# Layer 0's attention in written order on every engine, with the norm, the ranking and the adapter merges in other units

## The chip, the cores and the metric

The kernel runs on one core of a Trainium2 chip, in one launch. Its time is the device time of the whole launch in microseconds (us). Most of the work is matmuls on TensorE (PE). The other engines are VectorE (DVE), ScalarE (ACT), GpSimd (POOL) and SyncE (SP), which here issues the large loads and stores.

## The reference

The model has two layers, each an attention and a feed-forward part, each followed by a residual sum and a layer norm. The change lies in the first attention and in the preparation of the first feed-forward part. Eight batches of 512 rows of 512 numbers go through:

```python
x = _layernorm(x + attn0(x))        # 16 heads of 32, causal softmax, biases on Q, K, V and O
x = _layernorm(x + ffn0(x))         # 8 experts, the best 2 of each row
...
q = (x @ WQ_w.T + WQ_b); k = (x @ WK_w.T + WK_b); v = (x @ WV_w.T + WV_b)
attn = softmax(where(causal, -inf, q k^T / sqrt(32)));  out = (attn @ v) @ WO_w.T + WO_b
...
gate_delta = 2.0 * (gate_lora_B @ gate_lora_A)
probs = softmax(xf @ gate_weight.T + xf @ gate_delta.T); the top 2, their weights divided by their sum
gup = xf @ gate_up_proj[e] + 2.0 * (xf @ gup_lora_A[e].T) @ gup_lora_B[e].T
h = silu(gates) * h
out = h @ down_proj[e] + 2.0 * (h @ down_lora_A[e].T) @ down_lora_B[e].T
```

The adapters (lora A and B) have rank 16. All of it is float32. The second layer (attention with 8 heads on 2 key groups, then an integer feed-forward part) is the same code before and after the change.

## The kernel before, in words

`attention0` runs the first attention, batch by batch, b = 0 to 7. A batch has four groups g of four heads, and a group has three units u, `UNITS`: u = 0 takes the key tile 0 (512 query columns), u = 1 the key tiles 1 and 3 (384 + 128 columns), u = 2 the key tile 2 (256 columns). In each slot (g, u) the loop does the following, in this order:

1. `scores`: PE multiplies K and Q into the one buffer `sc`, ACT takes the exponential into `p`, POOL sets what lies above the diagonal to zero (affine_select).
2. the thunks that `plan(b)` has put into this slot's list.
3. `product` of the unit before (PE, `av`), and for u > 0 the adds of its p into a running sum (DVE).
4. in u = 1 `normalise` of the group before: PE sums rows (`rs`), ACT copies and bounds them (`watch_sums`), DVE takes the reciprocal and multiplies (`aoT`), POOL keeps a guard sum (`watch_inverses`, `g_total`).

The thunks of a batch b are these. `value(b, t)` in g = 0: four matmuls, and DVE adds the bias while it empties PSUM. `query` and `key` of the next group in u = 1 and u = 2: DVE empties Q, ACT empties K. `project(b - 1, t)`, t = 0 to 3, in (1,0) to (1,2): the output projection of the batch before, a DVE add to x, and after t = 3 the whole `layernorm` (statistics on DVE, the power on POOL, four subtract-and-multiply operations on DVE, four stores to `rows`). `turn(b - 1, c)`, c = 0 to 3, in (2,1) and (2,2): four transposes each on PE, the copies in turn on DVE and ACT. `score` in (3,0) and `choose` in (3,1): router logits and the top two. `dispatch(b - 2)` in (0,2): the rank of each row within its expert; `one_hot` and `enter(b - 2)` in (1,1): 24 small DVE operations of one-hot rows and a set of matmuls into a table. `merge` in (2,0) and (3,0): two adapters' deltas (`delta`, f32, 16 rows of K at row groups of 32), a scaling on ACT and an add into the expert's weights on POOL (L749, L760, L762). There are 24 merges: 12 in b1 to b6, 12 after the last batch. The load of the next x stands at g = 3 and the add of the output bias to x (one POOL operation on 128x2048) at g = 2.

PSUM for everything small (`mm`) has two buffers that alternate; `sc` has one. `one_hot` and `x1T`, the turned x, share one buffer.

The order on each engine comes from a scheduler, save where `in_order(tc)` is entered: there the order of the program is kept, for PE alone unless other engines are named. Before the change that covers the first unit, and PE from g = 2 of the last batch to the end of the tail; `begun.close()` ends the first. The tail, after the last batch, runs the first tiles of the experts (`tiles.step`, a tile of 128 rows through one expert), between them the rest of the last batch's projection, turn, score, choice, dispatch and one-hot rows, and the 12 remaining merges.

## Time and profile before

| | us |
|---|---|
| median of 3 runs | 2297.77 (2293.88 to 2298.08) |
| the profiled execution | 2295.71 |
| its span, first to last instruction | 2293.9 |
| mean granted clock | 0.994 |
| batches of layer 0's attention | 0 to about 735 |
| tail with the first expert tiles | 735 to about 850 |
| experts | to about 1190 |
| second attention | 1190 to 1776 |
| integer feed-forward part | 1780 to 2294 |

All numbers of the profile come from one execution. A line of the timeline has the start, the time from the first to the last of a group of like instructions, the engine, the line of the program, the operation, output and inputs by their names, and in brackets the idle time of the engine just before and what ended it. A matmul's own time is longer than the distance between two of them in a row, because they overlap; the cost of one is read from start to start. In windows, a row has the stretch, its length, then busy time and instructions of PE, weight loads, DVE, ACT and POOL, then the granted clock of PE, the share of DMA and GB/s.

### The profile page before, as it was taken

The page shows a single profiled execution, that of the slowest core. Times are in us where ns is not written, and L with a number is a line of the kernel's source. Part 1 is how long each engine was busy: PE and PEld are TensorE (multiplying, and loading weights), DVE is VectorE, ACT ScalarE, POOL GpSimd, SP SyncE. Part 2 cuts the span into 40 slices and gives each one's busy share as a digit, 9 for nine tenths or more (in the row PEclk, how much of TensorE's full clock was granted, in tenths as well). Part 3 has the DMA queues.
Part 4 walks back from the last instruction along what each step waited for, and adds up shares of the span by engine and source line. Part 5 has one row for each costly group of instructions (what it writes and reads, how often), then busy time and mean ns, then how long its engine had stood idle before and what let it go on. Part 6 is the DMA issues. An engine that isn't in the chain of part 4 may idle for free.

```text
span 2293.9 us, 24187 instructions
## 1 busy us (share of the span) xinstructions
PE 2240.5 (98%) x9430; PEld 1154.8 (50%) x9430; DVE 1245.0 (54%) x1974; ACT 648.2 (28%) x937; POOL 501.6 (22%) x493
## 2 busy tenths in 40 slices
PE   9999999999999999999998999999998999999997
PEld 3344444444444444444443334443343878888876
DVE  3457575666668432242216877777667544444443
ACT  2332323323324221111223323333332322222222
POOL 2231323413224231131125122321211000000000
PEclk9999999999999999999999999999999999999999
DMA  8010110101112234332233011100100100000000
GB/s 289 19 56 1 55 33 23 56 7 49 54 38 84 92 115 146 93 120 91 87 127 94 10 55 56 55 29 17 37 1 23 42 19 19 19 19 19 19 19 20
DMA packets 58444, 126.63 MB, mean 55 GB/s; under 512 B 6210, under 2 KB 6210, under 8 KB 58322
## 3 DMA queue, kind: packets, MB, share of 16 engines
q1 hardware_dynamic: 47040, 89.32, 11.1%
q0 software_dynamic: 10560, 34.61, 5.2%
q8 instruction: 77, 1.26, 0.2%
q10 hardware_dynamic: 722, 1.07, 0.1%
q14 instruction: 45, 0.37, 0.1%
HBM read 89.59 MB, written 35.39 MB: 54 GB/s over the span
## 4 chain that ended last, share of the span: by engine, by line
PE 76%; issue 8%; DVE 7%; DMA 4%; POOL 4%; ACT 2%; POOLq 0%; SPq 0%; ACTq 0%; DVEq 0%
PE ps_f L1069 7%; PE ps_g L1055 6%; PE ps_u L1055 6%; PE ps_gu L845 5%; PE ps_o L1216 5%; PE ps_o L1551 5%; PE av L1601 5%; PE sc L1579 4%; PE ps_q L1503 4%; PE ps_q L1200 4%; PE ps_k L1208 4%; PE ps_v L1193 4%; PE av L1288 3%; PE sc L1264 3%; PE ps_y L862 2%
## 5 line engine op out<-in xcount | busy, mean ns | idle before, releaser
L845 PE MATMUL ps_gu<-experts,xrT 128*128 128x512 f32 (+1 forms) x520 | 248.6, 601 | 0.0
L1268 ACT ACTIVATE p<-sc 128x2048 f32<-128x2048 f32 (+1 forms) x96 | 152.9, 1593 | 189.0 <-PE sc L1264 182.1
L1273 POOL TENSOR_SCALAR_AFFINE_SELECT p<-p 128x512 f32<-128x512 f32 x128 | 92.1, 734 | 380.1 <-ACT p L1268 376.6
L1060 DVE SCALAR_TENSOR_TENSOR hT<-ps_u,vec,sg 128x512 f32<-128x512 f32 x88 | 65.8, 748 | 201.4 <-PE ps_u L1055 201.4
L1069 PE MATMUL ps_f<-ffn_w,h_half 128*128 128x512 f32 x672 | 169.4, 392 | 1.1 <-DVE h_half L1064 1.1
L934 POOL TENSOR_TENSOR g_total<-g_total,r_inv 128x512 f32<-128x512 f32 x64 | 89.7, 1402 | 361.4 <-DVE r_inv L1612 286.2
L1612 DVE RECIPROCAL r_inv<-r_inv 128x512 f32<-128x512 f32 x32 | 106.8, 3339 | 105.4 <-ACT r_inv L931 105.4
L1582 ACT ACTIVATE p<-sc 128x1024 f32<-128x1024 f32 x128 | 124.1, 1021 | 130.3 <-PE sc L1579 119.7
L1296 DVE TENSOR_TENSOR p<-p 128x1536 f32<-128x1536 f32 (+2 forms) x96 | 129.3, 1346 | 38.5 <-POOL p L1273 21.5
L1055 PE MATMUL ps_g<-x_high,ffn_w 128*128 128x512 f32 x352 | 141.5, 402 | 3.0 <-DVE x L1557 3.0
L1069 PEld LDWEIGHTS ps_f<-ffn_w,h_half 128*128 128x128 f32 x672 | 124.5, 188 | 33.7 <-DVE h_half L1064 7.2
L848 DVE TENSOR_TENSOR h<-ps_gu,h 128x256 f32<-128x256 f32 x67 | 28.4, 424 | 205.2 <-ACT h L847 205.2
L1055 PE MATMUL ps_g<-x_low,ffn_w 128*128 128x512 f32 x352 | 139.4, 396 | 0.0
L1055 PE MATMUL ps_u<-x_high,ffn_w 128*128 128x512 f32 x352 | 139.2, 395 | 0.0
L1055 PE MATMUL ps_u<-x_low,ffn_w 128*128 128x512 f32 x352 | 139.2, 395 | 0.0
L1579 PE MATMUL sc<-qT,kT 64*128 64x512 f32 x512 | 127.9, 618 | 1.0 <-ACT qT L1505 0.7
L862 PE MATMUL ps_y<-experts,hT 128*128 128x512 f32 (+1 forms) x272 | 127.9, 592 | 0.5 <-ACT hT L856 0.5
L1200 PE MATMUL ps_q<-experts 128*128 128x512 f32 x256 | 120.4, 611 | 4.4 <-DMA experts<-in_xT 4.4
L845 PEld LDWEIGHTS ps_gu<-experts,xrT 128*128 128x128 f32 x520 | 89.6, 192 | 68.0 <-issue 68.0
L1601 PE MATMUL av<-p,v 128*64 128x512 f32 x512 | 123.8, 605 | 0.0
L1193 PE MATMUL ps_v<-experts 128*128 128x512 f32 x256 | 116.3, 602 | 2.4 <-DVE v L1195 2.4
L1208 PE MATMUL ps_k<-experts 128*128 128x512 f32 x256 | 117.5, 602 | 0.2 <-ACT r_inv L931 0.2
(256 smaller groups left out, 3544.5 us busy)
## 6 DMA issues: line engine op xcount, KB each, us to landing
results<-y SPq DMA_DIRECT2D x68, 256.0 KB
x<-in_x SPq DMA_DIRECT2D x8, 1024.0 KB
experts<-in_gate_up SPq DMA_DIRECT2D x8, 1024.0 KB
rows<-x SPq DMA_DIRECT2D x32, 256.0 KB
x<-rows SPq DMA_DIRECT2D x8, 1024.0 KB
experts<-in_xT SPq DMA_DIRECT2D x7, 1024.0 KB
out<-x SPq DMA_DIRECT2D x28, 256.0 KB
ffn_i<-in_wq_ffn SPq DMA_DIRECT2D x11, 512.0 KB
```

What stands on the lines that cost most here:

```text
L845: mm = nc.tensor.matmul(ps, lhsT=xT[:, c, :], rhs=self.weights(i, c), start=c == 0, stop=c == ND - 1)
L862: self.nc.tensor.matmul(ps, lhsT=hT[:, c, :], rhs=self.weights(i, ND + c), start=c == 0, stop=c == self.NI - 1)
L1055: nc.tensor.matmul(ps, lhsT=w[:, ts(dc, P)], rhs=x[:, dc, :], start=(dc, i) == (0, 0), stop=(dc, i) == (ND - 1, 1))
L1069: self.nc.tensor.matmul(os[t], lhsT=h[:, ts(t, P)], rhs=self.weights(2 * NHID + c), start=(c, i) == (0, 0), stop=(c, i) == (NHID - 1, 1))
L1193: nc.tensor.matmul(ps, lhsT=xts[b][:, c, ts(t, P)], rhs=wv[:, c, :], start=c == 0, stop=c == ND - 1)
L1200: nc.tensor.matmul(ps, lhsT=wq[:, g, ts(c, P)], rhs=xts[b][:, c, :], start=c == 0, stop=c == ND - 1)
L1208: nc.tensor.matmul(ps, lhsT=wk[:, g, ts(c, P)], rhs=xts[b][:, c, :], start=c == 0, stop=c == ND - 1)
L1268: nc.scalar.activation(p, sc[:, :, :width], AF.Exp, scale=scale)
L1296: nc.vector.tensor_tensor(total[:, :, P * kt :], total[:, :, P * kt :], p[:, :, at : at + w], ALU.add)
L1579: nc.tensor.matmul(sc[:, j, :], lhsT=st["kT"][hs, ts(kt, P)], rhs=st["qT"][g][hs, :], start=True, stop=True)
L1582: nc.scalar.activation(p, sc, AF.Exp, scale=scale)
L1601: nc.tensor.matmul(st["av"][HD * j : HD * (j + 1), :], lhsT=st["v"][:, kt, HD * j : HD * (j + 1)], rhs=p[:, j, :], start=kt == 0, stop=kt ...
```

## The change

Layer 0's batches 0 to 6 are written in order for PE, DVE, ACT and POOL; the last batch keeps the manner of before. With it:

- `value` is emptied by DVE and ACT in turn, without a bias. `join_bias`, once in b0, multiplies V's bias with Wo (four f32 matmuls) and adds it to the row of O's bias; the softmax's rows sum to one, so that V's bias reaches the output in this way.
- `project` takes one t a slot from (1,0) to (2,0), with its statistics; `norm` follows in (2,1). `one_hot` is cut into halves, in (1,1) and (2,1), `enter` follows (2,2)'s product. The four `turn` of a batch stand together in (3,0), `score` in (3,1), `begin_choice` in (3,2), `end_choice` in the next batch's (0,0), and `dispatch` in (0,1).
- DVE's adds of a unit come ahead of the next unit's thunks; `watch_inverses` one unit later; the O bias is added to x in four POOL operations; the load of x moves to (3,1) of the batch before.
- Adapters are fetched in 16 parts of 128 rows by up to 512 columns (256 KB) through one buffer `raw`. `split_part` puts the upper float32r half of each value (ACT) and what remains (POOL, two operations) on separate rows, so that a `delta` is one float32r matmul with K = 64. Merges come last in their slot. Splits stand in b0, b4, b7 and, four of them, in the tail, where the last merges stand two to a step.

```diff
-                nc.sync.dma_start(out=self.lora_sb[32 * j : 32 * j + R, i, :], in_=ins.lora[i, j])
+                at = 2 * P // 4 * (j % 2)
+                nc.sync.dma_start(out=self.lora_sb[32 * j : 32 * j + R, i, :], in_=ins.lora[2 * i + j // 2, at : at + R])
...
         nc.scalar.activation(tmp, tmp, AF.Exp)
+
+        yield
         nc.vector.tensor_reduce(red, tmp, AX.X, ALU.add)
         nc.vector.reciprocal(red, red)
...
-    def load_lora(self, pool, i):
-
-        self.lora = pool.tile([P, LORA], F32, tag="lora", name=f"lora_{i}")
-        for j in range(4):
-            self.nc.sync.dma_start(out=self.lora[32 * j : 32 * j + R, :], in_=self.env.ins.lora[i, j])
+    def masks(self, pool, lane):
+
+
+
+        nc = self.nc
+        bits = pool.tile([P, 2], I32, name="l_bits")
+        self.low = pool.tile([P, 2], F32, name="l_low")
+        self.sign = pool.tile([P, 2], F32, name="l_sign")
+        for i, bit in enumerate((2 * R, R)):
+            nc.vector.tensor_scalar(bits[:, i : i + 1], lane, bit, None, ALU.bitwise_and)
+        nc.vector.tensor_copy(self.low, bits)
+        nc.vector.tensor_scalar(self.low, self.low, 1.0, None, ALU.min)
+        nc.vector.tensor_scalar(self.sign, self.low, -2.0, 1.0, ALU.mult, ALU.add)
+        self.parts = [(q, c) for q in range(E // 2) for c in range(LORA_PARTS)]
+
+    def fetch_part(self, pool):
+
+        if self.parts:
+            q, c = self.parts[0]
+            at, n = 512 * c, min(512, LORA - 512 * c)
+            self.raw = pool.tile([P, 512], F32, tag="raw", name="l_raw")
+            self.nc.sync.dma_start(out=self.raw[:, :n], in_=self.env.ins.lora[q, :, at : at + n])
+
+    def split_part(self, pool):
+        nc = self.nc
+        q, c = self.parts.pop(0)
+        if c == 0:
+            self.lora = pool.tile([P, LORA], F32R, tag="lora", name=f"lora_{q}")
+        at, n = 512 * c, min(512, LORA - 512 * c)
+        i = int(c in (1, 2))
+        high = pool.tile([P, 512], F32R, tag="r_inv", name="l_high", bufs=2)[:, :n]
+        nc.scalar.activation(high, self.raw[:, :n], AF.Copy, scale=self.sign[:, i : i + 1])
+        raw = self.raw[:, :n]
+        nc.gpsimd.tensor_scalar(raw, raw, self.low[:, i : i + 1], None, ALU.mult)
+        nc.gpsimd.tensor_tensor(self.lora[:, at : at + n], raw, high.bitcast(F32), ALU.add)
+
+        if (q, c) != (E // 2 - 2, LORA_PARTS - 1):
+            self.fetch_part(pool)
 
     def delta(self, ps, e, c):
-        j = 32 * (e % 4)
-        a, bt = lora_factors(self.lora[j : j + R, :], c)
+        j = P // 2 * (e % 2)
+        a, bt = lora_factors(self.lora[j : j + P // 2, :], c)
         self.nc.tensor.matmul(ps, lhsT=a, rhs=bt, start=True, stop=True)
...
-    def step(self):
+    def step(self, amid=lambda: None):
...
+        amid()
         self.down(i)
         self.turn_rows(i + 3)
...
-        experts.load_lora(work, 0)
+        experts.masks(work, router.lane_i)
+        experts.fetch_part(work)
...
             vs[t] = own.tile([P, D], F32, tag=f"v{t}", name=f"v{t}")
-            nc.vector.tensor_tensor(vs[t], ps, row[:, 0, :], ALU.add)
+            env.evacuate(t, vs[t], ps)
+
+        def join_bias():
+
+            bv = work.tile([P, ND, P], F32, tag="r_inv", name="bv", bufs=2)
+            nc.vector.tensor_copy(bv, vec[:, V_BV : V_BV + ND, None].to_broadcast([P, ND, P]))
+            ps = mm([P, D], "ps_bias")
+            for c in range(ND):
+                nc.tensor.matmul(ps, lhsT=bv[:, c, :], rhs=wo[:, c, :], start=c == 0, stop=c == ND - 1)
+            nc.vector.tensor_tensor(row, ps, row, ALU.add)
...
             nc.vector.tensor_tensor(xs[b][:, t, :], ps, xs[b][:, t, :], ALU.add)
+            if b >= NB - 2:
+                if t == NT - 1:
+                    env.layernorm(b, router.rows[S * b : S * (b + 1)])
+                return
+            if t == 0:
+                norms[b] = [small.tile([P, NT, n], F32, name=name) for n, name in ((6, "stats"), (2, "mv"), (1, "rstd"))]
+            stats, mv, rstd = norms[b]
+            nc.vector.bn_stats(out=stats[:, t, :], in_=xs[b][:, t, :])
+            nc.vector.bn_aggr(out=mv[:, t, :], in_=stats[:, t, :])
             if t == NT - 1:
-                env.layernorm(b, router.rows[S * b : S * (b + 1)])
-
+                nc.gpsimd.tensor_scalar(rstd[:, :, 0], mv[:, :, 1], LN_EPS, None, ALU.add)
+                nc.gpsimd.tensor_tensor(rstd[:, :, 0], rstd[:, :, 0], env.neg_half, ALU.pow)
+
+        def norm(b):
+            stats, mv, rstd = norms.pop(b)
+            for t in range(NT):
+                x = xs[b][:, t, :]
+                nc.vector.tensor_scalar(x, x, mv[:, t, 0:1], rstd[:, t, :], ALU.subtract, ALU.mult)
+                nc.sync.dma_start(out=router.rows[S * b + P * t : S * b + P * (t + 1)], in_=x)
+
+        norms = {}
...
+        choosing = {}
+
+        def begin_choice(b):
+            choosing[b] = router.choose(b, logits.pop(b), mm([P, NT, E], "ps_r"))
+            next(choosing[b])
+
+        def end_choice(b):
+            next(choosing.pop(b), None)
+
         def choose(b):
-            router.choose(b, logits.pop(b), mm([P, NT, E], "ps_r"))
+            begin_choice(b)
+            end_choice(b)
...
+        def add(u, p, acc):
+            total, _ = acc
             at = 0
             for kt in UNITS[u]:
                 w = S - P * kt
-                if u:
-                    nc.vector.tensor_tensor(total[:, :, P * kt :], total[:, :, P * kt :], p[:, :, at : at + w], ALU.add)
+                nc.vector.tensor_tensor(total[:, :, P * kt :], total[:, :, P * kt :], p[:, :, at : at + w], ALU.add)
                 at += w
 
         def normalise(b, g, acc):
...
             guard.watch_sums(rs, r_inv)
             nc.vector.reciprocal(r_inv, r_inv)
             nc.vector.tensor_tensor(aoTs[b][:, g, :], av, r_inv, ALU.mult)
-            guard.watch_inverses(r_inv)
-
+            watches.append(r_inv)
...
                     todo[g, 2].append(lambda nb=nb, ng=ng: key(nb, ng))
             pb, last = b - 1, b == NB - 1
             if b:
-                places = ((1, 0), (1, 0), (1, 1), (1, 1) if last else (1, 2))
+                places = ((1, 0), (1, 0), (1, 1), (1, 1)) if last else ((1, 0), (1, 1), (1, 2), (2, 0))
                 for t, slot in enumerate(places):
-                    todo[slot].append(lambda t=t: project(pb, t))
-                places = ((2, 0),) * 4 if last else ((2, 1), (2, 1), (2, 2), (2, 2))
-                for c, slot in enumerate(places):
-                    todo[slot].append(lambda c=c: turn(pb, c))
-                todo[(2, 1) if last else (3, 0)].append(lambda: score(pb))
-                todo[(2, 2) if last else (3, 1)].append(lambda: choose(pb))
-                if not last:
-                    todo[2, 0].append(merge)
-                    todo[3, 0].append(merge)
+                    todo[slot].insert(0, lambda t=t: project(pb, t)) if not last else todo[slot].append(lambda t=t: project(pb, t))
+            if last:
+                for c in range(ND):
+                    todo[2, 0].append(lambda c=c: turn(pb, c))
+                todo[2, 1].append(lambda: score(pb))
+                todo[2, 2].append(lambda: choose(pb))
+            elif b:
+                todo[2, 1].append(lambda: norm(pb))
+                todo[3, 0] += [lambda c=c: turn(pb, c) for c in range(ND)]
+                todo[3, 1].append(lambda: score(pb))
+                todo[3, 2].append(lambda: begin_choice(pb))
+                for slot in ((2, 0), (3, 0)):
+                    after[slot] = merge
+
+            for t, slot in enumerate(((0, 0), (0, 1), (1, 0), (1, 1)) if b else ((2, 0), (2, 1), (2, 2), (3, 0))):
+                todo[slot].append(lambda t=t: nc.gpsimd.tensor_tensor(xs[b][:, t, :], xs[b][:, t, :], row, ALU.add))
+            if b + 1 < NB:
+
+                todo[3, 1].append(lambda: load_x(b + 1))
             if b == 0:
                 todo[1, 0].append(lambda: router.merge_lora(mm([P, ND, E], "ps_wr")))
+            if b == 0:
+                todo[1, 2].append(join_bias)
+            early = (0, 0), (0, 2), (1, 0), (1, 2)
+            slots = {0: ((2, 1), (2, 2), (3, 1), (3, 2)), 4: early, 7: early}
+            for slot in slots.get(b, ()):
+                todo[slot].append(lambda: experts.split_part(work))
             if b > 1:
-                todo[0, 2].append(lambda: dispatch(b - 2))
-                todo[1, 1].append(lambda: enter(one_hot(b - 2, range(NT))))
+                todo[0, 0].append(lambda: end_choice(b - 2))
+                todo[0, 2 if last else 1].append(lambda: dispatch(b - 2))
+                if last:
+                    todo[1, 1].append(lambda: enter(one_hot(b - 2, range(NT))))
+                else:
+                    todo[1, 1].append(lambda: one_hot(b - 2, (0, 1)))
+                    todo[2, 1].append(lambda: rows.append(one_hot(b - 2, (2, 3))))
+                    after[2, 2] = lambda: enter(rows.pop())
             if last:
                 todo[1, 2].append(soon)
                 todo[2, 2].append(first_rows)
...
                 todo[3, 2].append(begin)
             return todo
 
...
-        begun.enter_context(in_order(tc))
+        begun.enter_context(in_order(tc, mybir.EngineType.DVE, mybir.EngineType.Activation, mybir.EngineType.Pool))
         query(0, 0)
         key(0, 0)
         order = phase.enter_context(ExitStack())
         waiting = summing = None
         for b in range(NB):
+            if b == NB - 1:
+                begun.close()
             todo = plan(b)
             for g in range(ND):
-                if g == 2:
-                    if b + 1 < NB:
-                        load_xT(b + 1)
-
-                    nc.gpsimd.tensor_tensor(xs[b], xs[b], row[:, 1:2, :].to_broadcast([P, NT, D]), ALU.add)
-                if g == 3 and b + 1 < NB:
-                    load_x(b + 1)
+                if g == 2 and b + 1 < NB:
+                    load_xT(b + 1)
                 if b == NB - 1 and g == 1:
-                    experts.load_lora(work, 1)
                     experts.load(4)
                 if b == NB - 1 and g == 2:
                     order.enter_context(in_order(tc))
...
                 acc = []
                 for u in range(len(UNITS)):
                     p = scores(b, g, u)
+                    while watches:
+                        guard.watch_inverses(watches.pop())
+                    if waiting is not None and waiting[2]:
+                        add(*waiting[2:])
                     for thunk in todo[g, u]:
                         thunk()
-                    begun.close()
                     if waiting is not None:
-                        waiting()
+                        product(*waiting)
+                    after.pop((g, u), lambda: None)()
                     if u == 1 and summing is not None:
-                        summing()
-                    waiting = lambda b=b, g=g, u=u, p=p, acc=acc: product(b, g, u, p, acc)
-                summing = lambda b=b, g=g, acc=acc: normalise(b, g, acc)
-        waiting()
+                        normalise(*summing)
+                    waiting = b, g, u, p, acc
+                summing = b, g, acc
+        product(*waiting)
+        add(*waiting[2:])
         merge(2)
-        summing()
+        normalise(*summing)
+        guard.watch_inverses(watches.pop())
         heads_ctx.close()
         tiles.open(tiles_ctx)
         tiles.step()
...
             merge()
         for c in range(ND):
             turn(b, c)
+        experts.fetch_part(work)
         tiles.step()
         score(b)
         merge()
...
         dispatch(b)
         for places in ((0, 1), (2, 3)):
             rows = one_hot(b, places)
+            experts.split_part(work)
             tiles.step()
-            merge()
+            experts.split_part(work)
         enter(rows)
         tiles.of_fixed = router.fixed(routes)
         while merges:
-            tiles.step()
+            tiles.step(merge)
             merge()
```

More of the change, by code (lines that the diff above doesn't have):

```diff
@@ L46 @@
 LORA = 3 * 512 + 256
+LORA_PARTS = 4
 EXPERT = UPS * 512
@@ L51 @@
 WIDEST = 2048.0
-V_BQ, V_BK, V_NS, V_SS, V_SG, V_SU = 0, 4, 8, 12, 16, 16 + NHID
-N_VEC = 16 + 2 * NHID
+V_BQ, V_BK, V_NS, V_SS, V_SG, V_SU, V_BV = 0, 4, 8, 12, 16, 16 + NHID, 16 + 2 * NHID
+N_VEC = V_BV + 4
 def in_order(tc, *engines):
@@ L427, in __init__ @@
         self.tiles = numbers("r_tiles", [N_FREE], [[1, N_FREE]])
-        i = tmp.tile([P, 1], I32, name="r_lane_i")
+        self.lane_i = i = tmp.tile([P, 1], I32, name="r_lane_i")
         nc.gpsimd.iota(i, pattern=[[0, 1]], base=0, channel_multiplier=1)
@@ L1164, in attention0 @@
         load_w(wv, 0)
-        row = work.tile([P, 2, D], F32, name="row")
-        nc.sync.dma_start(out=row, in_=ins.rows.partition_broadcast(P))
+        row = work.tile([P, D], F32, name="row")
+        nc.sync.dma_start(out=row, in_=ins.rows[1].partition_broadcast(P))
         load_w(wq, 1, others)
@@ L1307, in normalise @@
             nc.vector.tensor_tensor(aoTs[b][:, g, :], av, r_inv, ALU.mult)
-            guard.watch_inverses(r_inv)
+            watches.append(r_inv)
+        watches = []
         merges = [(e, c) for e in range(0, E, 2) for c in range(UPS)]
@@ L1351, in plan @@
             return todo
+        rows, after = [], {}
         tiles = Tiles(env, router, experts.w)
@@ L1360, in begin @@
         def begin():
-            pair = work.tile([P, 2, D], F32, tag="row", name="first_turned")
-            one = work.tile([P, S], F32, tag="logits", name="first_turned")
-            tiles.begin([pair[:, 0, :], pair[:, 1, :], one], work.tile([P, 256], F32, name="first_h"),
+            rooms = [work.tile([P, S], F32, tag=tag, name="first_turned") for tag in ("row", "logits", "raw")]
+            tiles.begin(rooms, work.tile([P, 256], F32, name="first_h"),
                         lambda name: mm([P, S], name))
@@ L1993, in _layout @@
                            rows("L0_ffn_down_lora_A")], axis=3)
+    lora = np.repeat(lora.reshape(E // 2, 2, 1, R, LORA), 4, axis=2).reshape(E // 2, P, LORA)
     return {
@@ L1999, in _layout @@
             [cols(a[n]) for n in ("L0_attn_WQ_b", "L0_attn_WK_b", "L1_attn_norm_scale", "L1_attn_split_scale",
-                                  "L1_ffn_s_gate", "L1_ffn_s_up")], axis=1),
+                                  "L1_ffn_s_gate", "L1_ffn_s_up", "L0_attn_WV_b")], axis=1),
         "rows": np.stack([a["L0_attn_WV_b"], a["L0_attn_WO_b"]]),
```

## The prediction

> **What bounds the kernel now.** I read the page first: busy shares and the chain that ended last.
>
> ```profile
> PE 2240.5 (98%) x9430; PEld 1154.8 (50%) x9430; DVE 1245.0 (54%) x1974; ACT 648.2 (28%) x937; POOL 501.6 (22%) x493
> PE 76%; issue 8%; DVE 7%; DMA 4%; POOL 4%; ACT 2%; POOLq 0%; SPq 0%; ACTq 0%; DVEq 0%
> ```
>
> TensorE (PE) is busy all the time; what other engines do counts only where PE stands still for it, or where a matmul itself changes. So I went to the windows of 50 us (PE busy is the second time of a row, the granted clock the third figure from the right).
>
> ```profile
> 300.00:350.00 50.00, 49.42 (x276) 21.49 (x275) 30.32 (x35) 17.61 (x20) 13.37 (x15) 1.00 0.19 64
> 700.00:750.00 50.00, 44.92 (x252) 19.56 (x251) 39.67 (x83) 19.98 (x30) 21.91 (x23) 0.93 0.29 85
> 750.00:800.00 50.00, 48.22 (x167) 23.25 (x166) 20.62 (x59) 13.21 (x24) 14.16 (x14) 0.97 0.27 95
> ```
>
> Layer 0's batches run at full clock with 0.6 us of 50 idle: a reordering has little idle time to win there. The end of layer 0 (700 to 800) has 7 us of idle and a clock below one. Third, PE's timeline, for the stalls that there are and for the cost of one piece:
>
> ```profile
> 417.92 1.02 PE L749 MATMUL ps_lora<-lora 16*128 16x512 f32 x4
> 418.88 0.64 PE L1288 MATMUL av<-p,v 128*32 128x256 f32 x8
> 420.08 1.15 PE L1264 MATMUL sc<-q,k 32*128 32x384 f32 x16 [0.57 <-ACT p L1268]
> ...
> 463.72 2.84 PE L1193 MATMUL ps_v<-experts 128*128 128x512 f32 x6 [1.01 <-DVE v L1195]
> ...
> 699.07 1.09 PE L1228 MATMUL ps_x1T<-ident,x 128*128 128x128 f32 x8 [0.44 <-DVE g_routed L565]
> 701.11 1.15 PE L1228 MATMUL ps_x1T<-ident,x 128*128 128x128 f32 x8 [0.94 <-ACT x1T L1230]
> ```
>
> One merge of adapters takes 0.96 us from start to start; V waits 1.01 us for VectorE's (DVE's) evacuation; four transposes in a row, as the last batch has them already, stall 1.4 us. Last, DVE's timeline, for durations:
>
> ```profile
> 409.26 3.34 DVE L1306 RECIPROCAL r_inv<-r_inv 128x512 f32<-128x512 f32 x1
> 412.52 2.83 DVE L1296 TENSOR_TENSOR p<-p 128x512 f32<-128x512 f32 x2
> ...
> 419.77 4.14 DVE L153 TENSOR_SCALAR x<-x,mv,rstd 128x512 f32<-128x512 f32 x4 [1.48 <-POOL rstd L151]
> 424.90 0.75 DVE L1202 TENSOR_SCALAR q<-ps_q,vec 128x512 f32<-128x512 f32 x1 [1.00 <-PE ps_q L1200]
> ```
>
> **The batch's own sum.** Batches start (first V matmul) at 83.6, 174.4, 267.9, 360.7, 453.9, 547.9, 641.3 us: 90.7 us for b1, 93.4 as the mean of b2 to b6. From start to start in PE's timeline: V, Q, K, O 3.53 each, 16 of them 56.5; scores 1.07 + 1.08 + 0.65 by four groups 11.2; products 0.88 + 1.00 + 0.57 by four 9.8; row sums 4 x 0.98 = 3.9; rank 0.46, table 1.84, four transposes 2.1, logits 1.0, ps_r 0.89; together 87.7. Two merges are 2.22 before (eight records of two batches' 4.44). That leaves 3.4 us of 93.4: about 1.2 stalls (rows above) and about 2.1 that the transposes and merges cost over their length where the scheduler splits them among products and scores.
>
> **Merges in float32r.** Each delta becomes one record of 64 rows in place of two of 16. Price: the last layer's float32r matmul on 512 columns (L1069) repeats every 0.227 us, so a pair is estimated at 0.46 us, if the two don't overlap. Two merges 0.92: the sum is 88.65, and with 0.35 for the POOL select that PE waits for in batch 0 (61.76 us), 89.0. V's wait goes: its evacuation alternates now between DVE and ScalarE (ACT).
>
> **The turn, b2 to b6.** This is the number that decides. All four transposes now stand in (3,0), behind the table, and the table behind the norm and the second half of the one-hot rows in (2,1). DVE in its new order, from Q's end in (2,1): semaphore 0.2, q 0.7, norm four at 0.54 = 2.15, 12 one-hot operations 2.55 (24 took 5.07 from 482.40), reciprocal 3.3, aoT 0.64, adds of unit 1 2.23, table copy 0.92: 12.7 us. PE over the same stretch: product 0.88, row sums 0.98, scores 0.65, K 3.53, product 1.00, table 1.84, scores 1.07, first transpose 0.53: 10.5. With two buffers for the small products, the second transpose waits for the table's copy: 2.2 us. The third waits for the first's copy, which stands behind unit 2's add (1.17) on DVE and takes 0.68 itself; less the second's 0.53 on PE that is about 1.2. Uncontended S = 3.3. But POOL works beside DVE: the norm took 4.14 for 2.15 beside POOL, the adds 2.83 for 2.23. I take half of the norm's excess and the adds' and a little on the one-hots: S = 4.75. Ends: 1.4 (the last batch's turn, above), 6.2 (all contention in full).
>
> The clock bears on it. Here full stretches of 3.41 us at half clock follow loose ones, from 721.3, 738.4, 789.6 and 799.8 us; each costs some 1.7. A stall of 4.75 us cut by transposes is looser than anything in 50 to 700. I price one at 1.7 x 0.5 = 0.8 a batch; ends 0 and 1.7. So 89.0 + 4.75 + 0.8 = 94.55 against 93.4: +1.15 a batch, **+5.8 for five**.
>
> The Trainium skill (TensorE: Matmul & The Clock Gate, part "Why this matters for your kernels") wants no gaps over about 3 us between bursts, since one idle window of 3.4 us halves the clock. Its period agrees with the 3.41 us of the trace. The same rule taken strictly would charge the turn no clock, as transposes break the stall into 2.2 and 1.2 us, and make the sum 4 us less; the window 710 to 720, with PE 8.24 of 10 us busy, came before a halved one here, so I keep 0.8.
>
> **b1** has no table and rank, so 86.4 + 0.35 + a turn of 1.7 to 2.9 for the copies: about 89.0 against 90.7, **-1.7**.
>
> **b0.** The V bias leaves the evacuation and comes in through Wo: four f32 matmuls, 3.5 us, all on PE, with copy and add on DVE beside. In written order the three groups' 384+128 scores now wait for the 1.88 us exp in front, which Q's halves filled before: 0.73 + 1.49 + 1.49 = 3.7. Q unsplit gives 0.84 back, the select 0.35: **+6.0** (5 to 7.5).
>
> **b7, g0 and g1.** Four splits (a 256 KB load, ACT 0.6, POOL two operations of about 1.3 each by the row of the merge's add, L762). Behind the split's copy on ACT stands k's evacuation, and its part's load stands in SP's queue behind the 1 MB load of expert 4, itself waiting for PE's last V; 1 MB took 7 to 8 us at 434 us. PE then waits for k at the next score: 2 to 5 us if so, chance 0.6; with one halved stretch likely behind it **+3.5** (0 to 7). Splits in b0 and b4 have their loads an entire unit ahead: nothing, and where late, ACT would hold an exp.
>
> **The tail.** Twelve merges by 0.5: -6.0. The two merges in a burst (733.58 to 738.13, 4.55 us with two waits of 0.51) shrink by 2. One halved stretch fewer: -1.7. Against it four splits in series, each load, ACT, POOL about 6 us, ACT's hT and silu queued behind their copies: +3 (0 to 5). Merges of two a step: POOL 5.2 plus a gather 1.0 = 6.2 against a step's 5.8, some tenths. Sum **-6.7** (-14 to 0).
>
> POOL's x add in four pieces, g_total a unit later, loads of x a unit later (a whole batch of cover for a 7 to 8 us load), rows stored from the norm at 256 KB each and choice split over two units: hidden under PE's 93 us a batch, as POOL is busy 15 of 50 us; where POOL is late, the select holds the product, 0.35 a time.
>
> **Sum:** 6.0 - 1.7 + 5.8 + 3.5 - 6.7 = +6.9 on the profiled execution's 2295.7 = 2302.6. The median of runs, 2297.8, lies 2.1 higher; from midway, 2296.7, I get **2303.6**.
>
> **Rivals.**
> 1. Faster: the turn stalls no more than 3.2 us a batch, clock included, as the 1.4 at 699 us speaks for. At 1.4 each batch takes 90.4, five give -14.9, and the time is 2283; at 3.2 it is 2292. It decides below 3.2, since the other terms sum to +1.1 and 0.2% is 4.6 us. Against it: DVE's 12.7 us against PE's 10.5, which holds without any contention. Chance 0.28.
> 2. No net change: S with its clock between 3.2 and 5.1, uncontended chain or little more: 2293 to 2302. Chance 0.20.
> 3. Slower by more: contention in full and a halved stretch every batch, 6.2 + 1.7 = 7.9: 96.9 a batch, +17.5 for five, 2315. For it: POOL runs adapters and sums beside DVE; against: POOL is lightly loaded in b2, b3, b5, b6. Chance 0.10.
> 4. The float32r merges don't run faster, records of 64 rows cost 0.46 each or the pair waits: 24 merges by 0.5 return, +12, 2315. The four-record 0.96 speaks for a price by records; the last layer's 0.227 against. Chance 0.05.
>
> **How the numbers follow.** My forecast, slower at 2298 to 2311 with most over 2302.4, has 0.37; slower in all 0.37 + 0.10 + 0.05 = 0.52. This kernel's runs tell about 0.2%, 4.6 us, from no change. The range leaves out the lower tip of rival 1 and the upper of 3 and 4: 2284 to 2316.
>
> **What the new profile would show.** In b2 to b6 a batch of 94 to 95 us, with two waits of 2 to 3 and 1 to 2 us in front of transposes, put to DVE's table and x1T copies; no wait on v; merge pairs of 0.46; b0 6 us longer; a wait for k in b7; half-clock stretches before 640 us. I am wrong if the turn's waits are under 3 us in sum, or if ACT, in written order, holds an exp for something I have not seen queued ahead of it.

## The result and the profile after

The changed kernel takes 2354.46 us (median of 4 runs, 2352.11 to 2356.31), the kernel before 2297.64 beside it: a ratio of 1.0247 with a 95% interval of 1.0230 to 1.0264. It is slower by 57 us. The forecast was 2303.6 with a range to 2316: the sign was right and the size wrong by a factor of eight.

The page of the changed kernel, busy shares and chain:

```profile
PE 2249.2 (96%) x9390; PEld 1163.1 (49%) x9390; DVE 1231.8 (52%) x1965; ACT 667.5 (28%) x969; POOL 532.4 (23%) x549
PE 76%; DVE 9%; issue 7%; DMA 3%; POOL 3%; ACT 2%; POOLq 0%; ACTq 0%; DVEq 0%; SPq 0%
```

PE is busy 9 us longer than before although it has 40 records fewer, and its share falls by two points. Both come from the same stretches. The windows of 50 us (columns as before) alternate:

```profile
300.00:350.00 50.00, 50.00 (x233) 20.74 (x232) 25.66 (x65) 12.89 (x15) 12.47 (x14) 1.00 0.00 1
350.00:400.00 50.00, 42.39 (x234) 19.07 (x232) 29.13 (x40) 15.09 (x19) 13.82 (x16) 0.86 0.18 64
```

Half of each batch has no idle time at all; the other half has 7.6 us of it and, at a granted clock of 0.86, some 14 us at half clock (a granted clock of 0.5). PE's timeline of b4 shows where:

```profile
451.97 3.70 PE L1264 MATMUL ps_o<-experts,aoT 128*128 128x512 f32 x8
455.60 0.64 PE L1364 MATMUL av<-p,v 128*32 128x256 f32 x8
459.51 0.50 PE L786 MATMUL ps_lora<-lora 64*128 64x512 f32 x1 [3.27 <-DVE x L1265]
460.78 0.79 PE L786 MATMUL ps_lora<-lora 64*128 64x512 f32 x1 [0.77 <-ACT scaled L797]
461.50 2.09 PE L1340 MATMUL sc<-q,k 32*128 32x384 f32 x16
463.52 5.47 PE L1248 MATMUL ps_q<-experts 128*128 128x512 f32 x8
...
482.14 0.66 PE L1294 MATMUL ps_x1T<-ident,x 128*128 128x128 f32 x4 [2.51 <-DVE r_table L562]
483.87 1.72 PE L1294 MATMUL ps_x1T<-ident,x 128*128 128x128 f32 x8 [1.08 <-DVE x1T L164]
```

Two waits a batch, the same in all of b1 to b6: 3.27 + 0.77 us in front of the merge's two deltas in (2,0), and 2.51 + 1.08 us in the turn in (3,0) (b1, which has no table, has one wait of 2.59 there). Behind the first the scores take 2.09 in place of 1.15 us and Q 5.47 in place of 3.6: half clock. The sum of the stretches at half clock in b1 to b6 is 71.7 us, where it was none before.

VectorE's timeline says why the merge waits:

```profile
443.43 3.35 DVE L1384 RECIPROCAL r_inv<-r_inv 128x512 f32<-128x512 f32 x1
455.70 0.69 DVE L1385 TENSOR_TENSOR aoT<-av,r_inv 128x512 f32<-128x512 f32 x1 [8.93 <-PE ps_o L1264]
456.31 2.54 DVE L1374 TENSOR_TENSOR p<-p 128x1536 f32<-128x1536 f32 x2
458.77 0.68 DVE L1265 TENSOR_TENSOR x<-ps_o,x 128x512 f32<-128x512 f32 x1
```

There is one aoT buffer. The multiply of the new batch's group 0, issued in (1,1), may not write it before the old batch's last projection has read it, and the change has moved that projection to (2,0). VectorE stands 8.93 us, in order, with the adds and projection 2's evacuation (the add that empties its PSUM buffer) queued behind it; the evacuation ends at 459.45, and the merge needs that buffer. The adds stand ahead of the evacuation because the change has moved them ahead of the slot's thunks.

In b0 there is a third wait. Its releaser is named "issue", which is no cause; the end of VectorE's copy of bv (58.48 to 58.90) is:

```profile
59.00 6.32 PE L1242 MATMUL ps_bias<-experts,bv 128*128 128x512 f32 x8 [4.06 <-issue]
```

Lengths of the batches, from one first V matmul to the next ("rest" goes from b7's first V to the end of the span), and the time at half clock in b1 to b6:

| profiled kernel | b0 | b1 | b2 to b6, mean | rest | half clock | median of runs, us | ratio to before |
|---|---|---|---|---|---|---|---|
| before | 68.2 | 90.7 | 93.4 | 1652.6 | 0 | 2297.64 | |
| changed | 81.3 | 98.0 | 102.4 | 1647.1 | 71.7 | 2354.46 | 1.0247 |
| e1, projections early | 81.4 | 91.4 | 95.4 | 1644.7 | 30.7 | 2312.95 | 1.0072 |
| e2, the wait filled | 81.0 | 96.4 | 101.3 | 1645.9 | 44.4 | 2346.43 | 1.0216 |
| e13, adds behind projections | 81.1 | 96.7 | 99.2 | 1646.8 | 44.4 | 2337.64 | 1.0185 |
| e11, adds behind the turn | 81.2 | 95.2 | 97.2 | 1644.7 | 37.5 | 2326.58 | 1.0136 |
| e4, bias spread early | 74.3 | 100.9 | 102.4 | 1643.7 | 78.5 | 2348.72 | 1.0226 |
| e7, order for PE alone | 85.7 | 89.1 | 92.2 | 1647.5 | 0 | 2300.77 | 1.0018 |
| e9, the same from b1 | 84.2 | 89.1 | 92.5 | 1644.9 | 0 | 2299.30 | 1.0007 |
| e6, old plan and order | 80.5 | 90.6 | 93.0 | 1643.8 | 0 | 2302.54 | 1.0026 |
| e3 = e1 + e11 | 81.1 | 88.7 | 90.9 | 1648.8 | 0 | 2289.98 | 0.9964 |
| e10 = e3 + e4 | 74.4 | 88.7 | 90.9 | 1646.2 | 0 | 2282.01 | 0.9942 |
| e8, joined, rows late | 74.3 | 89.1 | 95.1 | 1644.4 | 23.9 | 2301.25 | 1.0019 |
| e12, rows early | 74.3 | 89.1 | 89.8 | 1648.6 | 0 | 2277.44 | 0.9917 |

The ratios are to runs of the kernel before that were made beside each run (medians 2294.83 to 2297.64). The column "rest" holds 25 to 39 us of half clock that differ from one execution to the next, so differences of a few us in it say little.

So the change's 60.5 us of span are 13.1 in b0, 7.3 in b1, 45 in b2 to b6, and 5.5 gained behind (with 31.5 and 32.5 us of half clock there, before and after); the first V starts 0.5 later.

### The profile page after: what moved, and what is told of

The parts are those of the page before. It is cut to its first block, busy times and chain, and to the rows that moved or that the text cites. A ratio compares the mean times of both kernels' runs of the same rounds, so it can differ in the third digit from the quotient of the medians.

```text
span 2354.4 us, 24235 instructions
## 1 busy us (share of the span) xinstructions
PE 2249.2 (96%) x9390; PEld 1163.1 (49%) x9390; DVE 1231.8 (52%) x1965; ACT 667.5 (28%) x969; POOL 532.4 (23%) x549
## 4 chain that ended last, share of the span: by engine, by line
PE 76%; DVE 9%; issue 7%; DMA 3%; POOL 3%; ACT 2%; POOLq 0%; ACTq 0%; DVEq 0%; SPq 0%
PE ps_f L1107 7%; PE ps_g L1093 6%; PE ps_u L1093 6%; PE ps_q L1248 5%; PE ps_o L1264 5%; PE ps_v L1232 5%; PE av L1706 5%; PE ps_o L1656 5%; PE sc L1684 4%; PE ps_q L1608 4%; PE ps_gu L882 4%; PE ps_k L1256 4%; PE sc L1340 4%; PE av L1364 3%; PE ps_y L899 2%
## 5 line engine op out<-in xcount | busy, mean ns | idle before, releaser
L1349 POOL TENSOR_SCALAR_AFFINE_SELECT p<-p 128x512 f32<-128x512 f32 x128 | 83.8, 667 | 361.9 <-ACT p L1344 354.1
L972 POOL TENSOR_TENSOR g_total<-g_total,r_inv 128x512 f32<-128x512 f32 x64 | 83.6, 1306 | 358.4 <-DVE r_inv L1717 286.3
L1717 DVE RECIPROCAL r_inv<-r_inv 128x512 f32<-128x512 f32 x32 | 106.8, 3338 | 105.5 <-ACT r_inv L969 105.5
L1248 PE MATMUL ps_q<-experts 128*128 128x512 f32 x256 | 130.3, 656 | 4.4 <-DMA experts<-in_xT 4.4
L1384 DVE RECIPROCAL r_inv<-r_inv 128x512 f32<-128x512 f32 x32 | 107.1, 3348 | 27.1 <-ACT r_inv L969 27.0
L882 PEld LDWEIGHTS ps_gu<-experts,xrT 128*128 128x128 f32 x520 | 88.7, 190 | 63.8 <-issue 63.8
L1250 DVE TENSOR_SCALAR q<-ps_q,vec 128x512 f32<-128x512 f32 x32 | 24.0, 751 | 183.6 <-PE ps_q L1248 183.6
```

The source lines that it names most:

```text
L882: mm = nc.tensor.matmul(ps, lhsT=xT[:, c, :], rhs=self.weights(i, c), start=c == 0, stop=c == ND - 1)
L1248: nc.tensor.matmul(ps, lhsT=wq[:, g, ts(c, P)], rhs=xts[b][:, c, :], start=c == 0, stop=c == ND - 1)
```

## The experiments

### The wait of the merge

Theory: the last projection's place holds VectorE through the one aoT buffer. First e1, which moves only the projections (in this and the other edits, `...` marks lines left out):

```diff
-                places = ((1, 0), (1, 0), (1, 1), (1, 1)) if last else ((1, 0), (1, 1), (1, 2), (2, 0))
+                places = ((1, 0), (1, 0), (1, 1), (1, 1))
...
-                    todo[slot].insert(0, lambda t=t: project(pb, t)) if not last else todo[slot].append(lambda t=t: project(pb, t))
+                    todo[slot].insert(t % 2, lambda t=t: project(pb, t)) if not last else todo[slot].append(lambda t=t: project(pb, t))
```

The second pair of lines keeps the two projections of a slot in their order.

> The changed kernel, with the four projections of the batch before in (1,0), (1,0), (1,1), (1,1) in place of one a slot up to (2,0); nothing else. Theory: in the changed kernel the multiply into aoT of group 0, in (1,1), has to wait until the last projection has read the one aoT buffer, and that projection now stands in (2,0); VectorE keeps its order, so the evacuation of projection 2 and the adds stand 8.9 us behind it, and the merge in (2,0) waits 3.27 + 0.76 us for a PSUM buffer; the clock then falls to half. With the last projection ahead of that multiply the wait goes: 6 batches x 4.0 = 24 us, and of the half-clock stretches behind it (34 us in all) about half as much again in time, 14 to 17: 2354.5 becomes 2313 to 2320, a batch 95 to 96 us. Rival A, the adds which now stand ahead of the thunks are what the evacuation waits for, and they still stand there: under 10 us gained, 2345 or more. Rival B, the clock falls because of the float32r merges themselves or the lower load of PE, not because of the wait: the idle time goes but the half-clock stretches at the merges stay, about 2330.

Measured 2312.95 us, at the lower end of what the theory had (ratio to before 1.0072, 1.0044 to 1.0100): 41.5 us less for three projections moved by a slot or two. The merge's waits are gone from the trace; this is PE's row of e1 for the merge in b4:

```profile
434.77 0.50 PE L786 MATMUL ps_lora<-lora 64*128 64x512 f32 x2
```

A small wait is new against the changed kernel, 1.0 us for the exponential in (2,1) (0.6 in the kernel before), as no projection stands in (2,0) to fill it.

How much of the wait is the multiply's and how much the adds' that follow it? e13:

```diff
+                    late = 0 < b < NB - 1 and (g, u) in ((1, 2), (2, 0))
-                    if waiting is not None and waiting[2]:
+                    if waiting is not None and waiting[2] and not late:
                         add(*waiting[2:])
                     for thunk in todo[g, u]:
                         thunk()
+                    if late:
+                        add(*waiting[2:])
```

> The changed kernel, with VectorE's adds in (1,2) and (2,0) behind the thunks of the slot (as the product stood to its adds before the change), so that the evacuations of projections 2 and 3 stand ahead of them; the multiply into aoT, which waits for the last projection, still stands ahead of both. It tells how much of the merge's 4.0 us is the multiply's wait and how much the 2.5 us of adds that come between it and the evacuation. Theory: both; the first delta then waits for the multiply and the evacuation alone, 0.7 to 1.0 us in place of 3.27, the second 0.8 as before, and with no wait of over 1 us the half clock behind the merge goes: 6 x 2.4 = 15 us and some 10 to 17 for the clock, 2322 to 2330. If the multiply's wait alone made it (PE free, VectorE held to the end of the last projection in any case), the wait stays above 2.5 us: 2345 or more.

The wait fell as expected, 3.27 to 0.81 us: it takes both, VectorE held to the end of the last projection and 2.5 us of adds between; the adds are the larger part of the wait. The time, 2337.64 us (1.0185, 1.0165 to 1.0205), missed the expectation by 8 us, and the trace suggests where they went. PE's and VectorE's timelines of e13:

```profile
449.16 0.50 PE L786 MATMUL ps_lora<-lora 64*128 64x512 f32 x1 [0.81 <-DVE x L1265]
450.43 0.49 PE L786 MATMUL ps_lora<-lora 64*128 64x512 f32 x1 [0.77 <-ACT scaled L797]
...
471.61 1.12 PE L1294 MATMUL ps_x1T<-ident,x 128*128 128x128 f32 x4 [5.26 <-DVE r_table L562]
```

```profile
456.39 4.46 DVE L1283 TENSOR_SCALAR x<-x,mv,rstd 128x512 f32<-128x512 f32 x4
```

The turn's wait grew from 2.51 to 5.26 us: PE arrives sooner, and the norm, 1.91 us in the changed kernel, takes 4.46 here: the merge's adds and three selects run on GpSimd beside it, from 456.33 to 461.35 us, where in the changed kernel GpSimd is idle through the norm. So 2.5 us were freed at the merge in each batch, and 2.3 of them came back at the turn (5.26 + 0.62 for 2.51 + 1.08); what e13 gained from b2 to b6, 3.2 us a batch, is nearly all clock.

### The clock

e2 leaves the wait as it is and fills it with work that nobody reads, four extra matmuls:

```diff
+        def fill():
+            sc = p_sc.tile([P, 4, S], F32, tag="sc", name="fill")
+            for j in range(4):
+                nc.tensor.matmul(sc[:, j, :], lhsT=wo[:, j, :P], rhs=wo[:, j, :], start=True, stop=True)
...
-                for slot in ((2, 0), (3, 0)):
-                    after[slot] = merge
+                after[2, 0] = fill_merge
+                after[3, 0] = merge
```

> The changed kernel, with four extra matmuls of 128x128 by 512 columns (3.5 us, into the score buffer, which is free then; their result is never read) on PE just ahead of the merge in (2,0), in b1 to b6. They do no useful work and fill the 3.27 us in which PE stands still there. Theory: the half clock comes from that idle stretch. The stretches of half clock behind the merge (34 us in all six batches) go, and the kernel gets faster by some 12 to 16 us although PE does 21 us more work: 2338 to 2343. Rival B, the clock falls for another reason (float32r, or total load): no gain, 2354 to 2358.

2346.43 us (1.0216, 1.0188 to 1.0244): with 21 us of useless work on PE the kernel is 8 us faster (2343.40 to 2348.31 against 2352.11 to 2356.31). No half-clock stretch follows the merge any more; PE's timeline of e2 in b4:

```profile
451.66 3.70 PE L1392 MATMUL fill<-experts 128*128 128x512 f32 x8
...
456.98 1.15 PE L1340 MATMUL sc<-q,k 32*128 32x384 f32 x16
...
475.86 0.76 PE L1294 MATMUL ps_x1T<-ident,x 128*128 128x128 f32 x4 [3.45 <-DVE r_table L562]
```

The scores behind the merge take 1.15 us again, not 2.09. That shows the clock's price by itself, and that the idle stretch sets it. The gain is less than the 12 to 16 expected since the turn's wait grew again, from 2.51 to 3.45 us, and the half clock behind the turn with it, from 37.5 to 44.4 us over b1 to b6.

### The turn

e11 (on the changed kernel) and e3 (on e1) put the adds of (2,2) and (3,0) behind the four transposes:

```diff
+                        adds.append(waiting[2:])
+                    turning = 0 < b < NB - 1 and (g, u) in ((2, 2), (3, 0))
+                    while adds and not turning:
+                        add(*adds.pop(0))
                     for thunk in todo[g, u]:
                         thunk()
+                    while adds and (g, u) != (2, 2):
+                        add(*adds.pop(0))
```

> The changed kernel, projections where it has them, with VectorE's adds of (2,2) and (3,0) behind the turn; nothing else. The turn's 3.6 us a batch should become 0.8, and the half clock behind it should go, while the merge's 4.0 us and its half clock stay: of the 71.7 us of half clock in b1 to b6, 34 are left. 5 x 2.8 + 1.8 = 16 us of waits and about half of 38, 12 to 19, together 28 to 35: 2320 to 2327. If the two waits only share one loss of clock: 2335 or more.

> The kernel with the early projections, and besides VectorE's adds of units 1 and 2 in (2,2) and (3,0) put behind the four transposes' thunks of (3,0). Theory: what the second and the third transpose wait for (2.5 and 1.1 us a batch) is the 3.1 and 1.2 us of adds that stand ahead of the table's copy and of the first x1T copy on VectorE; with the adds behind, the table's copy follows the table's matmuls at once. 3.6 us become about 1.0 in b2 to b6, 2.6 become 0.7 in b1, and of the 31 us of half clock behind the turn most goes: 2313 becomes 2284 to 2294, a batch about 91. Rival A: the chain is the norm and the one-hot rows ahead, not the adds: the waits stay above 2.5 us, over 2305. Rival B: the adds, put off by 4 us, hold the next row sums or the single buffer of unit 1's p, and the wait moves there: 2300 or more with a new wait on rs or p.

e11: 2326.58 us (1.0136, 1.0120 to 1.0153), inside its 2320 to 2327. e3: 2289.98 us (0.9964, 0.9951 to 0.9977), faster than the kernel before, inside 2284 to 2294. In e3 the turn's waits are 0.35 and 0.45 us in every batch, from PE's timeline:

```profile
440.69 0.66 PE L1294 MATMUL ps_x1T<-ident,x 128*128 128x128 f32 x4 [0.32 <-DVE x1T L164]
441.79 0.66 PE L1294 MATMUL ps_x1T<-ident,x 128*128 128x128 f32 x4 [0.44 <-ACT x1T L162]
```

and no half clock is left in b1 to b6. Alone the two edits gain 41.5 and 27.9 us, together 64.5: close to the sum, 69.

### Batch 0

e4 issues the copy of V's bias on VectorE in (1,0) in place of (1,2):

```diff
-        def join_bias():
-
+        bvs = []
+
+        def spread_bias():
             bv = work.tile([P, ND, P], F32, tag="r_inv", name="bv", bufs=2)
             nc.vector.tensor_copy(bv, vec[:, V_BV : V_BV + ND, None].to_broadcast([P, ND, P]))
+            bvs.append(bv)
+
+        def join_bias():
+            bv = bvs.pop()
+
...
+                todo[1, 0].append(spread_bias)
                 todo[1, 2].append(join_bias)
```

> The changed kernel, with the copy that spreads V's bias over its tile on VectorE in slot (1,0) of batch 0 in place of (1,2), ahead of the adds. Theory: PE's idle 4.06 us at 55 us, which the profile puts to issue, is this copy, standing at 58.48 us behind the reciprocal, the multiply and the adds of VectorE's queue; it and the 6.8 us of half clock behind it go: 4 + 3.4 = 7, so 2347. Rival: the wait is for something else (the load of Wo, or a PSUM buffer): 2354.

2348.72 us (1.0226, 1.0197 to 1.0254). b0 falls from 81.3 to 74.3 us, which is the 4.06 and most of the 3.4 that half clock over 6.83 us costs. Of these 7.0 the whole kernel keeps 5.7: b1 is longer, 100.9 for 98.0, with 17 us of half clock in place of 10.

### What the order is worth, and the rest of the change

e7 leaves DVE, ACT and POOL to the scheduler and keeps PE's order; e9 does so from b1 on; e6 keeps the plan, order and scheduler of before, with V's bias through Wo, float32r adapters, splits and the new tail. The edit of e7:

```diff
-        begun.enter_context(in_order(tc, mybir.EngineType.DVE, mybir.EngineType.Activation, mybir.EngineType.Pool))
+        begun.enter_context(in_order(tc))
```

> The changed kernel, with the written order kept for PE alone in batches 0 to 6; the scheduler orders VectorE, ScalarE and GpSimd as it did before the change. Theory: the waits come from VectorE's written order, and the scheduler puts the evacuations ahead of the multiply into aoT that has to wait: the merge's wait falls from 4.0 to under 1 us, 2310 to 2330. Rival C: PE's own order (merge right behind the last projection, four transposes together behind the table) makes the waits whatever VectorE's order is: 2345 to 2360.

2300.77 us (1.0018, 1.0005 to 1.0031), less than expected: with the same order on PE no half clock is left in b1 to b6, and b2 to b6 take 92.2 us. VectorE's timeline of e7 in b4:

```profile
425.56 0.68 DVE L1265 TENSOR_TENSOR x<-ps_o,x 128x512 f32<-128x512 f32 x1
...
431.68 0.69 DVE L1385 TENSOR_TENSOR aoT<-av,r_inv 128x512 f32<-128x512 f32 x1 [4.50 <-PE ps_o L1264]
```

The multiply still waits for the last projection, 4.50 us, but projection 2's evacuation now stands ahead of it, and the merge does not wait for it. So PE's order alone does not make the waits; by this trace it is VectorE's written order, together with the places, that does.

> PE alone in written order, as in the run before with the other engines left to the scheduler, but from b1 on; batch 0 is ordered by the scheduler on every engine save for its first unit. Theory: batch 0's loss (85.7 us against 68.2 before the change) is the written order of a batch that has no projection to fill the waits for the exponential, POOL's select and K; the scheduler brings it to 72 to 75 with the bias's 3.5 us in it: 2301 becomes 2287 to 2291. Rival: the bias matmuls and their wait make the loss: 2297 or more.

2299.30 us (1.0007, 0.9996 to 1.0019), in the rival's range. The theory fell: b0 is no better with the scheduler (84.2 us; 74.3 in written order with the copy early).

> The changed kernel's other parts alone: V's bias through Wo, the float32r adapters with their splits, and the tail, with the plan, the order and the scheduler's freedom of the kernel before. Theory: the written order and the new places cost all of the 57 us, and the rest of the change gains: per batch 1.3 us from the merges, some 5 us in the tail, against 4 to 6 us for the bias in b0: 2286 to 2294. Rival: splits and float32r merges cost time themselves (loads in SP's queue, POOL's 2.6 us a part): 2298 or more.

2302.54 us (1.0026, 1.0014 to 1.0038). This theory fell too: the rest of the change alone does not gain. A batch of b2 to b6 gains 0.4 us (93.0 for 93.4) and not the 1.3 expected. The column "rest" is 8.8 us shorter in the profiled execution, some 3 of it because less of it ran at half clock (25.4 us for 31.5); that execution, 2298.04 us, is the fastest of ten. And b0 loses 12.3. GpSimd's timeline of e6, and PE's:

```profile
57.03 2.48 POOL L777 TENSOR_SCALAR l_raw<-l_raw,l_low 128x512 f32<-128x512 f32 x1 [0.85 <-ACT l_high L775]
59.59 1.26 POOL L778 TENSOR_TENSOR lora<-l_raw,l_high 128x512 fp32r<-128x512 f32 x1
60.81 8.99 POOL L1449 TENSOR_TENSOR x<-x,row 128x2048 f32<-128x2048 f32 x2
69.74 1.83 POOL L1332 TENSOR_SCALAR_AFFINE_SELECT p<-p 128x512 f32<-128x512 f32 x3
```

```profile
70.45 1.12 PE L1347 MATMUL av<-p,v 128*32 128x512 f32 x8 [4.08 <-POOL p L1332]
...
82.03 1.14 PE L1323 MATMUL sc<-q,k 32*128 32x512 f32 x8 [2.38 <-ACT k L1258]
```

The row of biases exists only after the bias matmuls, so the scheduler issues the x adds of two batches together, 9 us, ahead of the select for which PE waits; and k's evacuation stands behind a split's copy that waits for its load. In b0 of the changed kernel, in written order with x added in four pieces behind the selects, neither wait is there. That the parts need an order like the new one is read from these traces; no run mends b0 under the old order.

### A version that beats both

e10 joins e1, e11 and e4; e8 and e12 do so too and also move the table into (2,0), to fill the 1.0 us for the exponential there, and the first merge to (2,2). In e8 the second half of the one-hot rows stands in (1,2), in e12 the halves stand in (0,2) and (1,1). What e12 adds to e10:

```diff
-                    todo[1, 1].append(lambda: one_hot(b - 2, (0, 1)))
-                    todo[2, 1].append(lambda: rows.append(one_hot(b - 2, (2, 3))))
-                    after[2, 2] = lambda: enter(rows.pop())
+                    todo[0, 2].append(lambda: one_hot(b - 2, (0, 1)))
+                    todo[1, 1].append(lambda: rows.append(one_hot(b - 2, (2, 3))))
+                    after[2, 0] = lambda: enter(rows.pop())
...
-                for slot in ((2, 0), (3, 0)):
+                for slot in ((2, 2), (3, 0)):
                     after[slot] = merge
```

> Early projections, adds behind the turn, V's bias spread in (1,0) of b0, and besides the second half of the one-hot rows in (1,2), the table behind (2,0) and the first merge behind (2,2). All engines keep the written order. Theory: no wait of over 1 us is left in b1 to b6; a batch comes to the sum of its matmuls, 89 to 90.5 us, b0 to 74: 2268 to 2282, faster than both kernels. Rival: the pieces meet elsewhere (the merge behind (2,2) against the transposes, the table's copy against the norm) and a batch stays at 92 or more: 2288 or more.

> Early projections, adds behind the turn, and V's bias spread in (1,0) of b0: the three single edits together, all engines in written order. If the three causes are apart from each other, b0 takes 74.3 us as where the bias alone was moved, and b1 to b6 88.7 and 90.9 as where the other two were: 2290.0 less 6.8 = 2283 (2281 to 2286), 0.6% faster than the kernel before. Rival: the half clock at b0 moves to the next loose place and half of the gain is lost, 2287.

> The same, and the one-hot rows in (0,2) and (1,1), the table behind (2,0), the first merge behind (2,2). Theory: in the joined version of the earlier call the table came too early for VectorE, whose second half of rows stood behind the adds in (1,2); with the rows ahead of the reciprocal the table fills the 1.0 us in which PE waits for the exponential of (2,0): a batch of 89.9 in place of 90.9, 2278 (2275 to 2281). Rival: the 2.6 us of rows ahead of the reciprocal in (1,1) make VectorE late for the next row sums or adds, a new wait takes the gain back: 2284 or more.

e8 went the rival's way, 2301.25 us (1.0019, 1.0009 to 1.0029): the rows, issued behind the adds in (1,2), come late. PE's timeline of e8:

```profile
237.39 0.27 PE L560 MATMUL ps_table<-one_hot 128*128 128x256 bf16 x1 [1.86 <-DVE one_hot L551]
237.97 0.37 PE L560 MATMUL ps_table<-one_hot 128*128 128x256 bf16 x1 [0.31 <-DVE one_hot L551]
```

Here half clock came from 237.7, behind 1.86 us of waiting. Such waits (1.84 to 2.53 us, and pieces of 0.2 to 0.3) came with half clock in four of the five batches b2 to b6, and in b5 without. e10: 2282.01 us (0.9942, 0.9928 to 0.9955), e12: 2277.44 us (0.9917, 0.9903 to 0.9931), both within their expectation. A batch of e12 from b2 on takes 89.8 us, with no wait above 0.45 us.

## Why the prediction was wrong, point by point

- **The batch's own sum, 88.65 plus 0.35.** Nearly right as work: e12's batches come to 89.8 with 0.8 us of waits, so 89.0. A pair of deltas was put at 0.46; the trace gives 0.72 (486.53 to 487.25), before 0.96. V's wait went, as forecast.
- **"The sum is 88.65" with no wait at the merge: this step failed.** The move of the last projection from (1,2) to (2,0) was not costed at all, nor were, at the merge, the adds that now stand ahead of the evacuation. It should have been followed past VectorE's queue: who waits for the last projection (the multiply into the one aoT buffer), and what stands behind that. The profile of before showed the dependence, in a line of VectorE's timeline that the prediction did not use:

```profile
416.05 0.69 DVE L1307 TENSOR_TENSOR aoT<-av,r_inv 128x512 f32<-128x512 f32 x1 [0.70 <-PE ps_o L1216]
```

  With the projection a slot later the 0.70 became 8.93, and the queue behind it cost PE 4.0 us in each of six batches. The prediction's own signs of being wrong did not show it: the turn's waits are over 3 us in sum, and no exponential is held in b1 to b6.
- **The turn, S = 4.75.** The mechanism was right and the size near: 3.6 us measured, by the table's copy and the first x1T copy as described; the uncontended 3.3 was the better value, since the norm took 1.91 and not 4.14. Beside GpSimd's adds and selects the norm took 4.14 before the change and 4.46 in e13; in the changed kernel GpSimd was idle then.
- **The clock, 0.8 a batch: mis-sized.** b2 to b6 have 61.4 us of half clock, 12 a batch, at half speed some 6. Of 102.4 us, 89.1 are work (e3's 90.9 less its 1.8 of waits), 4.0 and 3.6 the waits, the remaining 5.7 the clock. The two waits, some 20 us apart, each set it off (e11 and e1 each keep one of them, with 37.5 and 30.7 us of half clock).
- **b1, -1.7:** +7.3, by the same wait, 10.2 us of half clock and a turn near the top of its 1.7 to 2.9 (2.59).
- **b0, +6.0:** +13.1. The 3.5 of bias matmuls and the waits for the exponential (0.66, 1.43, 1.43) were in it; "copy and add on DVE beside" failed: the copy stood 4.06 us late behind the reciprocal and the adds, with 6.83 us of half clock.
- **b7 +3.5 and the tail -6.7:** together -5.5 for -3.2, measured to the end of the span. K's evacuation did stand behind a split's copy (732.19), but its load had landed in time and PE did not wait. In the tail a hT copy behind a split held PE 2.81 us at 882.6, once.
- **Rivals.** None was it: the wait that decided was in no rival. Rival 4, that float32r merges are no faster, was half right: of the 0.5 expected of a merge 0.24 came (0.96 to 0.72), and e6 has 93.0 for 93.4 a batch.

The Trainium skill (TensorE: Matmul & The Clock Gate, part "Why this matters for your kernels") asks for no gaps over about 3 us. The prediction weighed a strict reading of it, by which the turn would cost no clock. The runs decide against that reading. In e1 no wait of b1 to b6 is over 2.87 us, and there is half clock at the turn in every batch from b1 to b6 (30.7 us): in b1 one wait of 2.60 us was enough, and from b4 on it begins before the first of the two waits ends. In e8 waits of 1.84 to 2.53 us ahead of the table's matmuls came with it in four batches of five. Waits of 0.35 and 0.45 us at the turn did not set it off (e3, and e7 from b2).

## What to carry to other kernels

When a step is moved later, look for everyone who waits for its end, among them whoever is to write a single buffer that the step still reads, and then for what stands behind that waiter in an in-order queue. When idle time on a matmul engine at full clock comes together in one place, price the lost clock with it: here it cost about as much again (5.7 us a batch for 5.8 us more of waits than in e3). And a wait taken away can hand part of its gain to the next one, as in e2 and e13, whose turns waited longer; in e1 and e11 the other wait stayed as it was, and their gains nearly add up (e3).

## What the runs showed of the hardware

Filling an idle stretch of 3.3 us with work that nobody reads made the kernel faster (e2, by 8 us for 21 us more of matmuls). In layer 0's batches half clock comes in stretches that are multiples of 3.41 us, and up to 10.24 us in a row followed a turn. GpSimd's first operation of a split took from 1.56 to 3.07 us on the same 128x512 (e6); VectorE's norm took 1.91 us alone and 4.46 beside GpSimd.
